# Graph transformer over adjacency lists: paced steps, a pair's contexts turned one at a time, an earlier request for zT, a later flag, products of ones at the start, a last tile in two column halves

## The chip, the core and the metric

The kernel runs on one core of one Trainium2 chip. The metric is the device time of one execution in microseconds (us). The engines named below are PE (TensorE, with PEld for its weight loads), DVE (VectorE), ACT (ScalarE), POOL (GpSimd) and SP, whose queue issues transfers.

## The reference

Two layers of a graph transformer over 2708 nodes with 512 features, 8 heads of 64 and an inner width of 2048, all in float32. A node attends only to its neighbours in `adj` and to itself.

```
mask = adj + eye(n)
q, k, v = split_heads(h @ Wq.T + bq), split_heads(h @ Wk.T + bk), split_heads(h @ Wv.T + bv)
scores = where(mask == 0, -1e9, q @ k.T / 8)
ctx = softmax(scores) @ v
h1 = layer_norm(h + ctx @ Wo.T + bo, ln1_g, ln1_b)
out = layer_norm(h1 + relu(h1 @ W1.T + b1) @ W2.T + b2, ln2_g, ln2_b)
```

About nine of 2708 entries are set in a row, so nearly all scores are masked.

## The kernel before

`by_edges` (from L469) does the work; `by_rows` is a dense version that runs only if a flag, computed on the chip, says that the lists did not suffice.

**Tiles and blocks.** The nodes are sorted by how many neighbours they have and cut into 22 tiles of 128 rows; the last, tile 21, has 20 rows. `blocks` pairs them: (20, 19), (18, 17), (8, 9) and so on to (1, 16) and (21, 0). `order` is the same list, flat.

**Stages.** First come keys and values of all tiles in layer 0 (`first`), while DVE, ACT and POOL find each row's neighbours in `adj` (`lists`). Then come the queries of layer 0 (`first_queries`), with the first attention steps beside them. Then, for each layer, the eleven blocks go through the feed-forward part (`feed_forward`); layer 0 also makes keys and values of layer 1 for a finished block (`keys_values`), and at the change of layers PE makes layer 1's queries (`queries`, `query`).

**Attention** (`attend`, L1563) runs on POOL, DVE and ACT. A step takes two neighbours (SLOTS) of all rows of a tile: POOL gathers their key and value rows (L1095); DVE multiplies the keys by the query row and reduces by head (L1132, L1138); one step later ACT takes the exponent (L1151) and scales values (L1158), and DVE adds them (L1164, L1171). Two steps after a tile's last one come its sums, and three after it ACT divides and writes the context `cx` (L1202); the tile's number then stands in `got`, which holds at most three (CXB). A step that needs a query row fetches it (`asked`): by a gather on POOL from `q_d` in layer 0, by SP in layer 1.

**The feed-forward of a block** has 16 slices f of the inner width. PE makes `pf` (L1488, eight passes; a float32 product is two passes) into one of three PSUM banks, ACT applies the ReLU into `ft` (L1499), and three slices later (LAG) PE adds that slice's product into `a` (L1461). Between the slices stand, for the next block: turning its two contexts (`attended`: a transpose `tp` on PE at L1268 and a copy `cT` on ACT), the output product `o`, the first norm on DVE with a power on POOL (`rd`, L1258), and turning the result into `hT` (`turned`). A 20-row tile's products run in four quarters of the array (L597, L1476).

**Order.** All five engines are scheduled by hand: each runs its instructions strictly in the order in which the program text makes them. What interleaves attention with the rest is a pace. `advance(more)` (L1628) adds `more` to a credit of at most 1.5 and makes steps, each costing about its slots over two, while the credit is above zero and `got` has room. The tables `PACE` and `PACES` (the latter for a layer's first block) give `more` for each f; it is 0 for the first two to four slices and for two slices near f=11, where contexts are turned and norms run. `through(k)` makes steps until both tiles of block k stand in `got`.

```
credit = min(credit + more, 1.5)
while credit > 0 and len(got) < CXB:
    cost = next(ahead, None)
```

**Around the change.** At t = NT - 7 of the layer-0 queries, both contexts of block 0 are turned, and at t = NT - 6 their output products follow. At the start of layer 1 both are turned, then one query is made, then the output products. In every block both contexts of the next one are turned at f=10 (12 in the very first). `queries` asks SP for up to three tiles' `zT` (the transposed layer input) ahead of a query; in layer 1's block 0 it asks for tiles 21 and 0 at f=0, and their queries come at f=3 and f=7. `cT` and `zT` share three buffers. In layer 1's last block `checked` (f=8) and `settled` (f=11 and f=14) gather the flag: a product with `ones` (L1622), a comparison into `redo`, and a read of `redo` into a register. In that block the products into `a` wait until all ReLUs are done (`apart`), tile 21 first and tile 0 last; then come the addition (L1520), the norm (L1252 to L1262) and the store of tile 0.

Of the kernel before, what the change touches and what calls it, by code (L numbers as in the profile page):

```python
# [8 lines left out]
F32 = mybir.dt.float32  # L9
# [4 lines left out]
ALU = mybir.AluOpType  # L14
# [4 lines left out]
P = 128  # L19
DM = 512  # L20
# [5 lines left out]
NFC = FF // P  # L26
# [8 lines left out]
Q4 = 32  # L35
# [7 lines left out]
AHEAD = 10  # L43
XB, XBS = 256, 11
LEAD = 1.2
QT = 16
OWN = 5
LISTS = (4, 7, 9, 12, 13, 14, 15, 17, 18, 19)
EARLY = 3
PACES = (  # L50
# [429 lines left out]
def by_edges(ctx: ExitStack, tc: tile.TileContext, x, xT, adj, layers, out, redo):  # L480
# [9 lines left out]
    nc = tc.nc  # L490
    N = x.shape[0]
    NT = (N + P - 1) // P
# [28 lines left out]
    make_identity(nc, ident)  # L521
    ones = const.tile([P, P], F32, name="ones")
    nc.gpsimd.memset(ones, 1.0)
    mhalf = const.tile([P, 1], F32, name="mhalf")
    nc.gpsimd.memset(mhalf, -0.5)
    listed = const.tile([P, NT, 2 * LIST], F32, name="listed")
# [89 lines left out]
    def finish(steps):  # L616
        for _ in steps:
            pass
# [627 lines left out]

    def norm(z, r, gain, shift):

        st = small.tile([P, 6], F32, tag="st", name="st")
        nc.vector.bn_stats(st[:r], z[:r])  # L1252
        mv = small.tile([P, 2], F32, tag="mv", name="mv")
        nc.vector.bn_aggr(mv[:r], st[:r])
        va = small.tile([P, 1], F32, tag="va", name="va")
        nc.vector.tensor_scalar(va[:r], mv[:r, 1:2], EPS, None, ALU.add)  # L1256
        rd = small.tile([P, 1], F32, tag="rd", name="rd")
        nc.gpsimd.tensor_tensor(rd[:r], va[:r], mhalf[:r], ALU.pow)  # L1258
        nc.vector.scalar_tensor_tensor(
            z[:r], z[:r], mv[:r, 0:1], gain[:r], ALU.subtract, ALU.mult  # L1260
        )
        nc.vector.scalar_tensor_tensor(z[:r], z[:r], rd[:r], shift[:r], ALU.mult, ALU.add)  # L1262
# [14 lines left out]
    class Layer:  # L1277
# [131 lines left out]
        def attended(self, block, got, xbs=None):  # L1409

            cTs, hs = [], []
            for g in block:
                r = size(g)
                cx = got.pop(g)
                cT = dn.tile([P, NC, P], F32, tag="cT", name="cT", bufs=3)
                flip(cx, r, cT[:, :, :r], self.bv)
                cTs.append((g, r, cT))
            xbs = xbs or self.residuals(block)
            yield
            for (g, r, cT), xb in zip(cTs, xbs):  # L1420
                o = project(lambda c: cT[:, c, :r], r, self.wo, "o")
                h = dn.tile([P, DM], F32, tag="h", name="h", bufs=4)
                nc.vector.tensor_tensor(h[:r], o[:r], xb[:r], ALU.add)  # L1423
                plus_rest(h[:r], o, r)
                if self.n == 0:
                    nc.vector.tensor_tensor(h[:r], h[:r], self.bo[:r], ALU.add)
                norm(h, r, self.g1, self.e1b2)
                hs.append(h)
                yield
            yield hs  # L1430
# [10 lines left out]
        def feed_forward(self, block, hs, hT):  # L1441
# [9 lines left out]
                ]  # L1451
                wide = [t.rearrange("p s (i w) -> p (s i) w", w=2 * P) for t in wide]

            def second(f, only=None):
                c0 = 0
                for g, a in zip(block, accs):
                    r = size(g)
                    if only not in (None, g) or r <= Q4:
                        c0 += r
                        continue  # L1460
                    nc.tensor.matmul(  # L1461
                        a[:r],
                        fts[f][:, c0 : c0 + r],
                        self.w2[f // 2][:, f % 2, :],
                        start=(f == 0),
                        stop=(f == NFC - 1),
                    )
                    c0 += r
# [44 lines left out]
            zs = []  # L1513
            for g, a, h in zip(block, accs, hs):
                r = size(g)
                if apart:
                    for f in range(NFC):
                        second(f, g)
                z = h
                nc.vector.tensor_tensor(z[:r], a[:r], h[:r], ALU.add)  # L1520
                plus_rest(z[:r], a, r)
                norm(z, r, self.g2, self.e2)
                if self.n == NL - 1:
                    put(out, ident_i[:r, g : g + 1], z[:r], "out")
                zs.append(z)
# [36 lines left out]
    now = Layer(0, layers[0])  # L1562
# [53 lines left out]
    def settled():  # L1616

        held = small.tile([P, 1], F32, tag="held", name="held", bufs=1)
        nc.vector.tensor_reduce(held, flags, AX.X, ALU.min)
        yield  # L1620
        pr = ps.tile([P, DM], F32, tag="g", name="pr")
        nc.tensor.matmul(pr[:1, :1], ones[:, :1], held, start=True, stop=True)  # L1622
        nc.vector.tensor_scalar(redo, pr[:1, :1], P - 0.5, None, ALU.is_lt)
        yield nc.values_load(redo[0:1, 0:1], min_val=0, max_val=1)

    credit = 0.0

    def advance(more):  # L1628

        nonlocal credit  # L1630
        credit = min(credit + more, 1.5)
        while credit > 0 and len(got) < CXB:
            cost = next(ahead, None)
            if cost is None:
                break
            credit -= cost

    def through(k):

        while blocks[k][-1] not in got:  # L1640
            next(ahead)

    got = {}
# [10 lines left out]
    def beside_queries(t):  # L1654

        if t in (8, 10, 12, 14):
            now.load_w1(t // 2 - 4, nc.gpsimd)
            now.load_w2(t // 2 - 4, nc.gpsimd)
        if t == 6:
            now.settle()  # L1660
        if t == 16:
            now.load_w1(4, nc.scalar)
            now.load_w2(4, nc.scalar)
        if t > OWN + 1:
            advance(0.65)
        if t == NT - 10:
            early[0] = now.residuals(blocks[0])
        if t == NT - 7:
            through(0)
            early[0] = now.attended(blocks[0], got, early[0])  # L1670
            next(early[0])
        if t == NT - 6:
            for _ in blocks[0]:
                next(early[0])
        if t == NT - 2:
            *_, early[0] = early[0]
            early[0] = early[0], now.turned(blocks[0], early[0])
# [6 lines left out]
    for n in range(NL):  # L1684
        last = n == NL - 1
        nxt = None if last else Layer(n + 1, layers[n + 1])
        if n > 0:
            streamed = now.queries(order[10:16])
            got = {}
            ahead = attend(n, got)  # L1690
            for _ in range(2):
                now.query(*pool.pop(0))
            next(ahead)
            both = now.two(order[8:10])
            pool += [(g, both[:, i]) for i, g in enumerate(order[8:10])]
            next(streamed)
            now.stores = nc.scalar
            while pool:
                if len(pool) < 5:
                    advance(0.65)  # L1700
                now.query(*pool.pop(0))
            for i, _ in enumerate(streamed):
                if i == 1:
                    both = now.two(order[16:18])
                if i == 4:
                    now.stores = nc.sync
                if len(got) < 2 or i < 3:
                    advance(0.65)
            through(0)
            early[n] = now.attended(blocks[0], got)  # L1710
            next(early[n])
            now.query(order[16], both[:, 0])
            for _ in blocks[0]:
                next(early[n])
            streamed = now.queries(order[18 : 2 * AHEAD])
            next(streamed)
            now.query(order[17], both[:, 1])
            advance(0.6)
            next(streamed)
            advance(0.6)  # L1720
            *_, hs = early[n]
            early[n] = hs, now.turned(blocks[0], hs)
            finish(streamed)
            now.apart = False
            now.load_w2(NFC // 2 - 1)
        hs, hT = early[n]
        projecting = xbs = None
        for k, block in enumerate(blocks):
            more = k + 1 < NB
            asking = iter(())  # L1730
            if n > 0 and k + AHEAD < NB:
                asking = now.queries(blocks[k + AHEAD])
            for f, zs in enumerate(now.feed_forward(block, hs, hT)):
                if f == NFC:
# [3 lines left out]
                if more and n == 0 and f == 5 + 2 * (k == 0):  # L1738
                    xbs = now.residuals(blocks[k + 1])
                if more and f == 10 + 2 * (k + n == 0):  # L1740
                    through(k + 1)
                    projecting = now.attended(blocks[k + 1], got, xbs)
                    xbs = None
                    next(projecting)
                if more and f == 11 + 2 * (k + n == 0):
                    *_, hs_next = projecting
                if more and f == NFC - 1:
                    finish(asking)
                    hT = now.turned(blocks[k + 1], hs_next)
                advance((PACE if k else PACES)[n][f])  # L1750
                if f in (0, 3, 7, 9):
                    next(asking, None)
                if k == 0 and len(now.w1) < NFC // 2 and f % 2 == 0:
                    now.load_w1(len(now.w1), nc.scalar)
# [2 lines left out]
                    now.load_second(1, temp)  # L1757
                if last and not more and f == 8:
                    checked()
                if last and not more and f == 11:  # L1760
                    settling = settled()
                    next(settling)
                if last and not more and f == 14:
                    again = next(settling)
                if not more and f == 0:
                    finish(ahead)
# [99 lines left out]
```

## Time and profile before

| | |
|---|---|
| median of 3 runs | 1864.73 us (1863.62 to 1865.01) |
| the profiled execution's own time | 1866.47 us |
| its span, first to last instruction | 1864.4 us |
| mean granted PE clock | 0.994 |
| DMA, mean over the span | 197 GB/s |

The profile shows one execution. Its groups give a line, an engine, an operation, the tiles written and read, a count, the busy time and the mean of one. A PE row's duration reaches until its result is out, while the next product starts earlier: passes of 512 columns start 0.43 us apart and are listed with 0.59 us each. The waits view sums, for an engine, what ended its idle time. The windows view gives busy time, the granted clock and DMA of a stretch. Where the names are not enough, the timeline gives each instruction's start, duration and, in brackets, the idle time before it and its releaser.

### The profile page before, as it was taken

To read this page: it belongs to the slowest core of one execution; us is meant where nothing else is said; L and a number is where in the kernel's file an instruction comes from. 1 tells how busy PE (TensorE), PEld (TensorE's weight loads), DVE (VectorE), ACT (ScalarE), POOL (GpSimd) and SP (SyncE) were. 2 spreads that over 40 slices of the span, in tenths; PEclk is the share of its full clock that TensorE was granted. 3 is DMA by queue.
4 is the path that set the end of the run, shared out by engine and by line. 5 is a ranking of instruction groups with operands and counts; after the bars stand their busy time and mean duration, and the time that the engine had idled before them with its cause. 6 is when DMAs were issued, how large, how long until landed. Compare 5 with 4: busy or idle time off the path is not lost.

```text
span 1864.4 us, 20896 instructions
## 1 busy us (share of the span) xinstructions
PE 1833.7 (98%) x6149; PEld 1088.4 (58%) x6149; DVE 1373.0 (74%) x2145; ACT 944.3 (51%) x3263; POOL 778.2 (42%) x745
## 2 busy tenths in 40 slices
PE   9999989999999999999999999999999999999997
PEld 3444446665656656566565644566666666666664
DVE  5886868777776867768674147878988998899842
ACT  5770535555555555455553113655655675666521
POOL 3234754443444534435430032434453654455302
PEclk9999989999999999999999999999999999999999
DMA  9997977545554565444631676826554664565300
GB/s 343 363 338 257 362 256 254 191 151 207 183 173 154 183 199 183 156 169 133 218 120 45 228 263 239 318 101 226 187 187 175 241 222 143 201 211 175 119 1 20
DMA packets 129829, 368.01 MB, mean 197 GB/s; under 512 B 14378, under 2 KB 32670, under 8 KB 129704
## 3 DMA queue, kind: packets, MB, share of 16 engines
q0 software_dynamic: 70608, 252.12, 39.4%
q1 hardware_dynamic: 50042, 93.64, 14.3%
q10 hardware_dynamic: 9054, 20.81, 2.9%
q8 instruction: 50, 0.82, 0.2%
q14 instruction: 75, 0.61, 0.1%
HBM read 315.84 MB, written 50.68 MB: 197 GB/s over the span
## 4 chain that ended last, share of the span: by engine, by line
PE 92%; DVE 3%; DMA 2%; issue 2%; ACT 1%; POOL 0%; ACTq 0%; SPq 0%; POOLq 0%; DVEq 0%
PE pf L1488 31%; PE a L1461 31%; PE k L602 8%; PE v L602 8%; PE o L602 7%; PE q L602 4%; PE tp L1268 3%; PE a L1476 1%; DMA kv<-kv_d,listed 1%; DMA zT<-zT_d 1%; DVE kv L1132 0%; DVE sc L1138 0%; DMA q_d<-qs 0%; ACT kv L1158 0%; ACT cx L1202 0%
## 5 line engine op out<-in xcount | busy, mean ns | idle before, releaser
L1488 PE MATMUL pf<-hT,w 128*128 128x256 f32 (+1 forms) x2816 | 635.2, 373 | 10.0 <-ACT ft L1499 9.1
L1488 PEld LDWEIGHTS pf<-hT,w 128*128 128x128 f32 x2816 | 520.1, 191 | 185.1 <-issue 107.3
L1461 PE MATMUL a<-w,ft 128*128 128x512 f32 x1312 | 611.3, 592 | 0.0
L1095 POOL DMA_INDIRECT kv<-kv_d,listed x420 | 501.8, 1195 | 260.0 <-issue 111.9
L1499 ACT ACTIVATE ft<-pf,b 128x256 f32<-128x256 f32 (+1 forms) x336 | 153.8, 461 | 432.9 <-PE pf L1488 427.9
L1461 PEld LDWEIGHTS a<-w,ft 128*128 128x128 f32 x1312 | 247.2, 190 | 187.8 <-issue 166.7
L1258 POOL TENSOR_TENSOR rd<-va,mhalf 128x1 f32<-128x1 f32 (+1 forms) x88 | 81.4, 925 | 577.4 <-DVE va L1256 577.3
L1158 ACT ACTIVATE kv<-kv,p 128x64 f32<-128x64 f32 x1232 | 311.0, 335 | 5.0
L1132 DVE TENSOR_TENSOR kv<-kv,q 128x1024 f32<-128x1024 f32 (+1 forms) x222 | 257.1, 1158 | 10.6 <-DMA q<-q_d,ident_i 7.6
L1138 DVE TENSOR_REDUCE sc<-kv 128x16 f32<-128x1024 f32 (+1 forms) x222 | 258.0, 1162 | 7.6
L1171 DVE TENSOR_TENSOR acc<-acc,kv 128x1024 f32<-128x1024 f32 (+2 forms) x178 | 205.3, 1153 | 75.8 <-ACT kv L1158 61.4
L1151 ACT ACTIVATE p<-sc,listed 128x8 f32<-128x8 f32 x420 | 104.7, 300 | 143.9 <-DVE sc L1138 114.5
L1164 DVE TENSOR_TENSOR kv<-kv,p 128x512 f32<-128x512 f32 (+1 forms) x178 | 122.6, 689 | 60.2 <-ACT p L1151 45.2
L602 PE MATMUL o<-wo,cT 128*128 128x512 f32 x336 | 148.0, 593 | 0.0
L602 PEld LDWEIGHTS o<-wo,cT 128*128 128x128 f32 x336 | 63.7, 190 | 81.1 <-issue 76.6
L727 DVE MAX8 tops<-code 128x8 f32<-128x247 f32 (+2 forms) x242 | 78.6, 400 | 28.9 <-ACT code L722 28.7
L1262 DVE SCALAR_TENSOR_TENSOR h<-h,rd,ln_b 128x512 f32<-128x512 f32 (+1 forms) x88 | 66.1, 751 | 42.2 <-POOL rd L1258 42.2
L1202 ACT ACTIVATE cx<-acc,su 128x64 f32<-128x64 f32 (+1 forms) x352 | 88.3, 333 | 13.2 <-DVE su L1194 7.4
L1158 ACT ACTIVATE acc<-kv,p 128x64 f32<-128x64 f32 (+1 forms) x352 | 88.8, 335 | 1.4
L602 PE MATMUL k<-wk,xg 128*128 128x512 f32 x168 | 78.0, 608 | 4.6 <-DMA wk<-in_Wk 4.6
L722 ACT ACTIVATE code<-aj 128x1354 bf16<-128x1354 int32 (+1 forms) x44 | 72.8, 1720 | 18.9 <-POOL aj L716 13.4
L1423 DVE TENSOR_TENSOR h<-o,xb 128x512 f32<-128x512 f32 (+1 forms) x44 | 30.2, 686 | 62.7 <-PE o L602 38.9
(179 smaller groups left out, 1524.4 us busy)
## 6 DMA issues: line engine op xcount, KB each, us to landing
aj<-in_adj SPq DMA_DIRECT2D x42, 677.0 KB
kv_d<-kvs ACTq DMA_DIRECT2D x21, 512.0 KB
xg<-in_xT SPq DMA_DIRECT2D x19, 512.0 KB
w<-in_W SPq DMA_DIRECT2D x16, 512.0 KB
kv<-kv_d,listed POOLq DMA_INDIRECT x420
zT_d<-zT SPq DMA_DIRECT2D x22, 256.0 KB
xb_d<-h SPq DMA_DIRECT2D x21, 256.0 KB
q<-q_d SPq DMA_DIRECT2D x21, 256.0 KB
```

Of the source, the lines that this page charges most:

```text
L602: nc.tensor.matmul(o[:r], xs(c), wm[:, c, :], start=(c == 0), stop=(c == NC - 1))
L1095: return nc.gpsimd.indirect_dma_start(out=to, out_offset=None, in_=table[:, :], in_offset=bass.IndirectOffsetOnAxis(ap=s, axis=0), bounds_ ...
L1132: nc.vector.tensor_tensor(kv[:r, :c, :DM], kv[:r, :c, :DM], self.q[:r].unsqueeze(1).to_broadcast([r, c, DM]), ALU.mult,)
L1138: nc.vector.tensor_reduce(self.sc[:r, s0 : s0 + c, :], kv[:r, :c, :DM].rearrange("p s (h d) -> p s h d", d=DK), AX.X, ALU.add,)
L1151: nc.scalar.activation(p[:r, s, :], self.sc[:r, s, :], AF.Exp, bias=minus[:r, g, s : s + 1])
L1158: nc.scalar.activation(to[:, i, hd], kv[:r, i, DM + h * DK : DM + (h + 1) * DK], AF.Copy, scale=p[:r, s0 + i, h : h + 1],)
L1164: nc.vector.tensor_tensor(to[:, 0, :].rearrange("p (h d) -> p h d", d=DK), kv[:r, 0, DM:].rearrange("p (h d) -> p h d", d=DK), p[:r, s0, : ...
L1171: nc.vector.tensor_tensor(self.acc[:r, :c, :], self.acc[:r, :c, :], kv[:r, :c, DM:], ALU.add)
L1202: nc.scalar.activation(cx[:r, hd], self.acc[:r, 0, hd], AF.Copy, scale=self.su[:r, h : h + 1])
L1461: nc.tensor.matmul(a[:r], fts[f][:, c0 : c0 + r], self.w2[f // 2][:, f % 2, :], start=(f == 0), stop=(f == NFC - 1),)
L1488: nc.tensor.matmul(pf[:, :w], self.w1[f // 2][:, c, f % 2 * P : f % 2 * P + P], hT[:, c, :w], start=(c == 0), stop=(c == NC - 1),)
L1499: nc.scalar.activation(ft[:, :w], pf[:, :w], AF.Relu, bias=self.b1[:, f : f + 1])
```

## The change

Seven edits. `advance` returns at once for a pace of 0, so that left-over credit makes no step there. `through(k)` becomes `until(g)`, for one tile, and `attended` yields after each of its two turns: the first context is turned at f=10 (12), the second one slice later, directly ahead of the output products. In layer 0's queries the first is turned at t = NT - 8, and the second and the output products at NT - 7; at the start of layer 1 one query comes between the two turns. The request for `zT` of tiles 21 and 0 moves ahead of the query of tile 16, which precedes the feed-forward. The flag's reduction moves from f=11 to f=10, its product from f=14 to f=12, and the read stays at f=14. Twelve products of `ones` with itself are put ahead of the keys. The very last tile's products are made in two halves of 256 columns, each with its own addition and statistics.

```
+WARM = 12
...
+    pr = ps.tile([P, DM], F32, tag="g", name="pr")
+    for _ in range(WARM):
+        nc.tensor.matmul(pr[:, :P], ones, ones, start=True, stop=True)
...
-    def norm(z, r, gain, shift):
+    def norm(z, r, gain, shift, st=None):
-        st = small.tile([P, 6], F32, tag="st", name="st")
-        nc.vector.bn_stats(st[:r], z[:r])
+        if st is None:
+            st = small.tile([P, 6], F32, tag="st", name="st")
+            nc.vector.bn_stats(st[:r], z[:r])
...
                 cTs.append((g, r, cT))
-            xbs = xbs or self.residuals(block)
-            yield
+                if g == block[0]:
+                    xbs = xbs or self.residuals(block)
+                yield
...
-                if apart:
-                    for f in range(NFC):
-                        second(f, g)
+                if apart and r > Q4:
+                    st = small.tile([P, 2, 6], F32, tag="st2", name="st2", bufs=1)
+                    for i in range(2):
+                        cols = slice(i * DM // 2, (i + 1) * DM // 2)
+                        for f in range(NFC):
+                            second(f, g, cols)
+                        nc.vector.tensor_tensor(z[:r, cols], a[:r, cols], h[:r, cols], ALU.add)
+                        nc.vector.bn_stats(st[:r, i], z[:r, cols])
...
         nc.vector.tensor_scalar(redo, pr[:1, :1], P - 0.5, None, ALU.is_lt)
+        yield
         yield nc.values_load(redo[0:1, 0:1], min_val=0, max_val=1)
...
     def advance(more):
+        if not more:
+            return
...
-    def through(k):
-        while blocks[k][-1] not in got:
+    def until(g):
+        while g not in got:
             next(ahead)
...
-        if t == NT - 7:
-            through(0)
+        if t == NT - 8:
+            until(blocks[0][0])
             early[0] = now.attended(blocks[0], got, early[0])
             next(early[0])
-        if t == NT - 6:
+        if t == NT - 7:
+            until(blocks[0][1])
+            next(early[0])
             for _ in blocks[0]:
                 next(early[0])
...
             next(early[n])
             now.query(order[16], both[:, 0])
+            until(blocks[0][1])
+            next(early[n])
...
             early[n] = hs, now.turned(blocks[0], hs)
+            asking = now.queries(blocks[AHEAD])
+            next(asking)
             finish(streamed)
...
                 if more and f == 10 + 2 * (k + n == 0):
-                    through(k + 1)
+                    until(blocks[k + 1][0])
                     projecting = now.attended(blocks[k + 1], got, xbs)
...
                     next(projecting)
                 if more and f == 11 + 2 * (k + n == 0):
+                    until(blocks[k + 1][1])
                     *_, hs_next = projecting
...
-                if f in (0, 3, 7, 9):
+                if f in (0, 3, 7, 9) and (f or k):
                     next(asking, None)
...
-                if last and not more and f == 11:
+                if last and not more and f == 10:
                     settling = settled()
-                    next(settling)
-                if last and not more and f == 14:
+                if last and not more and f in (10, 12, 14):
                     again = next(settling)
```

More of the change, by code (lines that the diff above doesn't have):

```diff
@@ L1452, in feed_forward, with second @@
                 wide = [t.rearrange("p s (i w) -> p (s i) w", w=2 * P) for t in wide]
-            def second(f, only=None):
+            def second(f, only=None, cols=slice(0, DM)):
                 c0 = 0
@@ L1461, in second @@
                     nc.tensor.matmul(
-                        a[:r],
+                        a[:r, cols],
                         fts[f][:, c0 : c0 + r],
-                        self.w2[f // 2][:, f % 2, :],
+                        self.w2[f // 2][:, f % 2, cols],
                         start=(f == 0),
@@ L1515, in feed_forward @@
                 r = size(g)
-                if apart:
-                    for f in range(NFC):
-                        second(f, g)
[L1519 to L1522, printed above, removed]
+                z, st = h, None
+                if apart and r > Q4:
[6 more added lines that the diff above has]
+                        nc.vector.bn_stats(st[:r, i], z[:r, cols])
+                else:
+                    nc.vector.tensor_tensor(z[:r], a[:r], h[:r], ALU.add)
+                    plus_rest(z[:r], a, r)
+                norm(z, r, self.g2, self.e2, st)
                 if self.n == NL - 1:
@@ L1708, in by_edges @@
                     advance(0.65)
-            through(0)
+            until(blocks[0][0])
             early[n] = now.attended(blocks[0], got)
@@ L1729, in by_edges @@
             more = k + 1 < NB
-            asking = iter(())
-            if n > 0 and k + AHEAD < NB:
+            if k or n == 0:
+                asking = iter(())
+            if n > 0 and 0 < k < NB - AHEAD:
                 asking = now.queries(blocks[k + AHEAD])
```

## Prediction

> **What bounds the kernel now.** I read the page first: TensorE (PE) is busy for nearly the whole span.
>
> ```profile
> span 1864.4 us, 20896 instructions
> PE 1833.7 (98%) x6149; PEld 1088.4 (58%) x6149; DVE 1373.0 (74%) x2145; ACT 944.3 (51%) x3263; POOL 778.2 (42%) x745
> ```
>
> The change adds a few products and removes none, so it can gain only where PE stands still or runs slowly. Second, what PE waited for (total us, times, longest):
>
> ```profile
> PE pf L1488 <- ACT ft L1499: 9.1, 1, 9.1
> PE k L602 <- DMA wk<-in_Wk: 4.6, 1, 4.6
> PE tp L1268 <- ACT cx L1202: 2.9, 4, 1.3
> PE q L597 <- DMA zT<-zT_d: 2.7, 1, 2.7
> PE pf L1488 <- ACT fts L1499: 0.8, 1, 0.8
> ```
>
> Third, the same places in stages (length, PE, PEld, DVE, ACT, POOL busy, granted clock, DMA share, GB/s): after three of the waits PE goes on at half clock.
>
> ```profile
> 268.60:272.20 3.60, 3.54 (x8) 2.86 (x9) 3.56 (x7) 0.72 (x3) 2.52 (x4) 0.50 1.00 324
> 1144.00:1147.50 3.50, 1.81 (x9) 0.91 (x8) 2.32 (x6) 2.20 (x10) 0.00 (x0) 1.00 0.35 124
> 1180.50:1184.00 3.50, 3.50 (x13) 1.59 (x14) 3.43 (x5) 0.00 (x0) 2.57 (x2) 0.56 1.02 383
> 1214.20:1217.70 3.50, 3.50 (x10) 2.72 (x9) 2.06 (x3) 3.47 (x15) 0.00 (x0) 0.51 0.00 0
> ```
>
> Fourth, the largest wait in order of time, PE and then ACT, POOL, DVE:
>
> ```profile
> 257.66 1.88 PE L1461 MATMUL a<-w,ft 128*128 128x512 f32 x4
> 268.66 3.74 PE L1488 MATMUL pf<-hT,w 128*128 128x256 f32 x8 [9.12 <-ACT ft L1499]
> ...
> 273.95 1.89 PE L1488 MATMUL pf<-hT,w 128*128 128x256 f32 x8
> ```
> ```profile
> 252.68 0.47 ACT L1499 ACTIVATE ft<-pf,b 128x256 f32<-128x256 f32 x1 [1.31 <-PE pf L1488]
> ...
> 265.70 0.49 ACT L1151 ACTIVATE p<-sc,listed 128x8 f32<-128x8 f32 x2 [12.36 <-DVE sc L1138]
> ...
> 268.15 1.17 ACT L1499 ACTIVATE ft<-pf,b 128x256 f32<-128x256 f32 x3
> ```
> ```profile
> 259.67 1.01 POOL L1095 DMA_INDIRECT q<-q_d,ident_i  x1 [2.58 <-DMA bq<-in_bq]
> ```
> ```profile
> 263.19 1.23 DVE L1132 TENSOR_TENSOR kv<-kv,q 128x1024 f32<-128x1024 f32 x1 [7.56 <-DMA q<-q_d,ident_i]
> ```
>
> After slice f=0 of the first feed-forward the pace is 0, but left-over credit made two attention steps. They need tile 17's query row, gathered at 259.67 and there at 263.19. ACT, in order, stands at their exponent until 265.70, the ReLUs of f=1 to 3 behind it, and PE has no free pf bank.
>
> **Part by part.**
>
> *Zero pace.* In the changed program's order the two steps come after f=4, so ACT reaches the exponent behind ft of f=4. PE then runs on from 250.65: 1.73 us a slice for f=0 to 2, 3.45 from f=3 (273.95 to 277.39), so pf of f=4 ends at 261.0, of f=5 at 264.5. With the gather unmoved, ft of f=5 starts at 268.15, 3.7 late. By the same rows ft of f=6 comes after DVE's next reduction (269.3), 0.5 exponent, 2.0 scaling and 2.0 for cx: 273.9, 6.0 late; f=10 I find about 7 late. A ReLU may start 8.1 late before PE waits: three banks, so 3x1.72 + 2x1.73 until the bank is wanted, less 0.47. So no wait, with 1 us of margin. Gain 9.12 + (3.74 - 1.89) = 10.97. Two things move the gather: the weight DMAs of f=0 and f=2 are no longer held behind ACT: four of 512 KB, issued at 266.31 to 267.88 before, now go at about 253 to 256 beside the q_d stores, 2.1 MB at 385 GB/s, up to 5.4 us later; against that the norms of tiles 20 and 19 now precede a step's gathers on POOL, where DVE idled 2.83 us for rd (237.78), so the last q_d store leaves up to 2 us sooner. I keep 0.5 us of wait: -10.5, ends -11 and -5. Elsewhere a step slips by about one slice. Nothing waits for it: by the order both contexts of the next pair stand in `got` at f=10 of every block but layer 1's first, and the turn itself comes at f=10 and 11.
>
> *Contexts turned apart.* At layer 1's start PE turned tile 20, waited for tile 19's cx, then made a query; now the query (3.43) lies between. Wait 1.24 and a slow turn (1.76 for 0.60): -2.4. Its cover is that query; without it the 2.4 return. At t=15 of layer 0 the cT copy loses its cover: +0.2. In layer 1's block 0 both turns stood at f=10: they took 3.51 (1210.57 to 1214.08) for 0.88, then 3.40 for 1.89 and 2.10 for 1.88 at half clock, 4.36 lost. Now f=11's 3.45 lie between, but the first cT copy comes ahead of cx of tile 17 on ACT: 0.3 + 1.06 copy + 0.49 exponent + 2.02 + 2.0 cx + 0.1 = 5.97 from the first turn, against PE's 0.45 + 3.45 + 0.45 = 4.35: 1.6 still waited. Half clock may follow (+1.7) or not. I take 2.3 left: -2.1, ends -4.3 and 0. In other blocks cx is done a slice or more before.
>
> *zT sooner.* Wait 2.67, then 1.92 for 1.05 and 2.60 for 1.89 at half clock: 4.25. Both zT left SP at 1170.83 behind two q_d stores and 512 KB of weights. Now they follow the store that went at 1162.53; the second needs the slot that query 1 frees (PE, 1164.7). Even with the 9.6 us that the chain gives this DMA, the first lands by 1172.1, the second by 1174.3, and PE, 2.4 earlier, wants the first at 1175.4. SP holds two q_d stores and w2 behind that slot, whose evictions come at about that time anyway: 0. -4.2.
>
> [...]
>
> *Products of ones.* Twelve 128x128 products, 24 passes; ones is ready at 1.52, the first wk at 4.63. In the chain the first key tile's eight passes take 6.04, the next ones' 3.43; the rows between are half rate, with 0.85 between passes until 9.40. 24 passes at 0.218 (half of 512 columns' rate, 429 ns, is 0.858) last 5.1: to 6.9, or 6.5 if the clock comes sooner; they delay the keys by about 2 and spare the 2.4 to 2.6 that half rate costs. [...] -0.5, ends -1.5 and +0.8.
>
> *Flag later.* The 0.77 at 1838.44 is PE reading redo just after making it; now two slices lie between. -0.6, ends -0.8 and 0. Its product at f=12 waits for held, done at 1827.0.
>
> *Halves of the last tile.* The add and statistics after the last product go from 0.69 to an estimated 0.42 each (0.54 between the 512 and 1024 column adds, halved): -0.54. 64 passes at 0.216 for 32 at 0.429: +0.1. [...] +0.3, ends -0.4 and +0.8.
>
> Sum: -10.5 - 2.4 + 0.2 - 2.1 - 4.2 - 0.5 - 0.6 + 0.3 = -19.8. The profiled execution is 1866.47 (span 1864.4): 1846.7. It lies 1.7 above the median of 1864.73, so the median becomes 1844.9.
>
> **Rivals.** *The first wait moves instead of going.* For: ACT still stands at the same exponent, the 2.1 MB go earlier, and margins are 1 us. If the gather lands 5 us later, ReLUs f=6 and 10 start 11 to 12 late: about 4 us of waits, with clock 5 in all: 1850. Against: DVE's stores leave earlier. *Everything goes*, no residue at either place and a good clock window: 1841. *The change doesn't do what it says*: zT stays behind SP's store and the credit is spent elsewhere; the waits return one slice on: 1864. Against: the order shows both moved. *Slower:* DVE and ACT, relieved of nothing, now trail a PE that is 15 us ahead; two steps fall on the first paid slice (2 x 4.2 us of DVE) in every block. It decides once a ReLU is over 8.1 late. Two steps (1.16 + 1.16 + 0.69 + 1.15 each, by the groups of L1132, L1138, L1164 and L1171) on a ReLU that is 1 late make 9.4, so 1.3 of wait, in 18 blocks 23 us: 1844.9 + 23 = 1868. Against: the latest I found outside the first block are 6.3, with key products in between, and 5.9 (pf to 1645.4, the cx of 1649.34 before the ReLU); every block's start and end are back at 0.2, and the order doubles steps in few places.
>
> **Numbers.** Forecast 0.68 at 1844.9 (its own 1842 to 1848); moved wait 0.20 at 1850; all gone 0.07; no change 0.02; slower 0.03. Range 1841 to 1851. A measurement can tell 0.2%, 3.7 us: faster 0.95, same 0.02, slower 0.03.
>
> **What would show it.** No PE wait over 1 us in the first feed-forward and no half clock there; zT's wait gone; cx's left once, near 1.6, at layer 1's first f=11; one new wait of PE for DVE in the last tile; the first key tile near 3.6 but starting near 6.5. Wrong if waits for ft appear at f=6 to 10 or in later blocks.

## The result, and the profile after

| | before | changed |
|---|---|---|
| median | 1864.83 us (4 runs, one more than above) | 1847.65 us (1846.59, 1846.72, 1848.58, 1848.60) |
| profiled execution | 1866.47 us | 1846.72 us |
| its span | 1864.4 us | 1844.6 us |
| ratio of the medians | | 0.9909, 95% interval 0.9892 to 0.9926 |

The change makes the kernel 17.2 us faster. The profiled execution lies where the prediction's sum put it (1846.7); the median is 2.7 us above the 1844.9 that was made of it, inside the range. The page of the changed kernel, its first lines:

```profile
span 1844.6 us, 20998 instructions
PE 1830.8 (99%) x6205; PEld 1095.4 (59%) x6205; DVE 1374.6 (75%) x2147; ACT 944.3 (51%) x3263; POOL 782.5 (42%) x745
```

PE's waits in the changed kernel (total us, times, longest). Of the five lines of before, those for `ft` (9.1), `zT` (2.7) and `fts` (0.8) are gone; `cx` is left once with 0.7, and the wait for `wk` has become one for `ones` and 0.4 for `wk`. New are `cT` and L1529.

```profile
PE pr L527 <- POOL ones L524: 1.6, 1, 1.6
PE tp L1273 <- ACT cx L1206: 0.7, 1, 0.7
PE o L606 <- ACT cT L1278: 0.6, 1, 0.6
PE tp L1273 <- DVE h L1267: 0.6, 1, 0.6
PE a L1467 <- DVE h L1529: 0.5, 1, 0.5
PE k L606 <- DMA wk<-in_Wk: 0.4, 1, 0.4
```

The windows view of the same three places: the first feed-forward, the query of tile 21 and the second turn of layer 1's block 0. Its columns are length, busy time of PE, PEld, DVE, ACT and POOL, granted clock, DMA share and GB/s. The clock is 1.00 in all.

```profile
268.60:272.20 3.60, 3.60 (x14) 2.36 (x13) 3.53 (x8) 2.75 (x12) 2.83 (x3) 1.00 1.01 366
1163.50:1167.00 3.50, 3.50 (x19) 1.96 (x18) 3.36 (x5) 1.67 (x8) 2.46 (x3) 1.00 1.03 400
1196.00:1200.00 4.00, 2.87 (x9) 1.16 (x8) 1.23 (x2) 3.94 (x17) 0.00 (x0) 1.00 0.00 0
```

From here on, "lost" is counted on PE from the trace: the time from the start of one pass to the start of the next, less what such a pair of passes usually takes (0.429 us for 512 columns, 0.216 for 256). It holds waits, half clock and slow turns together.

The first feed-forward loses nothing in this execution, but by a hair. ACT reaches the exponent of the two steps at 261.57 and gets the scores at 266.66; the ReLUs trail from there on (timeline of the changed kernel, ACT):

```profile
261.20 0.47 ACT L1505 ACTIVATE ft<-pf,b 128x256 f32<-128x256 f32 x1 [3.03 <-PE pf L1494]
261.57 0.29 ACT L1155 ACTIVATE p<-sc,listed 128x8 f32<-128x8 f32 x1
266.66 0.49 ACT L1155 ACTIVATE p<-sc,listed 128x8 f32<-128x8 f32 x2 [4.80 <-DVE sc L1142]
...
290.13 0.46 ACT L1505 ACTIVATE ft<-pf,b 128x256 f32<-128x256 f32 x1
```

And PE:

```profile
290.20 0.60 PE L1273 MATMUL tp<-ident,cx 128*128 128x128 f32 x4
290.64 1.99 PE L1494 MATMUL pf<-hT,w 128*128 128x256 f32 x8
```

The ReLU of f=10 ends at 290.59 (the start and duration of its row above), and the slice f=13, which needs its bank, starts at 290.64.

### The profile page after: what moved, and what is told of

Same layout as the page of the kernel before. It is cut to its first block, busy times and chain, and to the rows that moved or that the text cites. A ratio compares the mean times of both kernels' runs of the same rounds, so it can differ in the third digit from the quotient of the medians.

```text
span 1844.6 us, 20998 instructions
## 1 busy us (share of the span) xinstructions
PE 1830.8 (99%) x6205; PEld 1095.4 (59%) x6205; DVE 1374.6 (75%) x2147; ACT 944.3 (51%) x3263; POOL 782.5 (42%) x745
## 4 chain that ended last, share of the span: by engine, by line
PE 93%; DVE 3%; ACT 1%; issue 1%; DMA 1%; POOL 0%; SPq 0%; POOLq 0%; DVEq 0%
PE pf L1494 30%; PE a L1467 29%; PE o L606 8%; PE v L606 8%; PE k L606 8%; PE q L606 7%; PE tp L1273 3%; DVE sc L1142 1%; DVE kv L1136 1%; PE a L1482 1%; ACT kv L1162 1%; DVE acc L1175 0%; DVE kv L1168 0%; ACT cx L1206 0%; DMA kv<-kv_d,listed 0%
## 5 line engine op out<-in xcount | busy, mean ns | idle before, releaser
L1099 POOL DMA_INDIRECT kv<-kv_d,listed x420 | 507.8, 1209 | 254.2 <-issue 108.7
L1560 ACT COPY kvs<-v 128x512 f32<-128x512 f32 (+1 forms) x22 | 12.9, 585 | 137.3 <-PE v L606 136.6
```

The source lines that it names most:

```text
L1099: return nc.gpsimd.indirect_dma_start(out=to, out_offset=None, in_=table[:, :], in_offset=bass.IndirectOffsetOnAxis(ap=s, axis=0), bounds_ ...
```

## The experiments

Unless it says otherwise, each kernel is the changed one with the edit shown. Since the same kernel differs by 1 to 4 us between executions, the places in the traces tell more than the medians.

**The changed kernel once more.** 

> The changed kernel itself once more, as what the other runs of this chip are to be compared with. Expected 1846.5 to 1849, 0.991 of before. Its profile is expected to show in the first feed-forward what the time tells: no PE wait there with a time near 1846.6, and a wait for ft of 1 to 2 with one near 1848.6.

Measured: 1848.16 us (1847.30 to 1851.03, 4 runs), 0.9899 of before (0.9885 to 0.9914). Its profiled execution, the one of 1851.03, lost 4.10 in the first feed-forward, more than expected. Its span is 4.4 longer than that of the first profile (1849.0 against 1844.6): 4.1 of this lies here, while the first value product comes 0.45 later. From POOL, DVE and PE of its timeline:

```profile
260.67 1.01 POOL L1099 DMA_INDIRECT q<-q_d,ident_i  x1 [4.63 <-DMA raw<-in_bo]
...
267.99 1.22 DVE L1136 TENSOR_TENSOR kv<-kv,q 128x1024 f32<-128x1024 f32 x1 [13.41 <-DMA q<-q_d,ident_i]
...
279.08 2.58 PE L1494 MATMUL pf<-hT,w 128*128 128x256 f32 x8 [1.90 <-ACT ft L1505]
```

Its windows, before and after the clock fell:

```profile
276.93:280.35 3.42, 1.52 (x7) 1.15 (x7) 3.28 (x5) 3.39 (x15) 0.99 (x1) 1.00 0.92 328
280.35:283.76 3.41, 3.41 (x7) 1.84 (x6) 3.27 (x5) 2.02 (x8) 2.65 (x3) 0.50 0.60 190
```

The same rows of the first execution, for comparison:

```profile
258.81 1.01 POOL L1099 DMA_INDIRECT q<-q_d,ident_i  x1 [4.20 <-DMA w<-in_W]
...
264.14 1.23 DVE L1136 TENSOR_TENSOR kv<-kv,q 128x1024 f32<-128x1024 f32 x1 [10.82 <-DMA q<-q_d,ident_i]
```

In the same program, the gather of tile 17's query row left 9.8 instead of 8.3 us after the feed-forward's first product (250.84 and 250.48) and took 7.3 instead of 5.3 to the multiplication that needs it. That is the rival "the first wait moves", and the wait of 1.90 stands at f=9, where the prediction's sign of being wrong has it (waits for ft at f=6 to 10).

**Later weights.** In layer 0's first block:

```
-                if k == 0 and len(now.w1) < NFC // 2 and f % 2 == 0:
+                if k == 0 and len(now.w1) < NFC // 2 and f % 2 == 0 and f > 3:
```

> The changed kernel with the three pairs of weight loads of layer 0's first block issued behind ft of f=4, 6 and 8 instead of f=0, 2 and 4. Theory (the two groups of the changed kernel's times, 2.0 us apart, come from its first feed-forward, where the ReLU of f=10 is 8.5 late with 0.1 to spare, and the weights' transfers beside tile 17's q_d store and gather set by how much): the gather leaves up to 1.5 us and lands up to 3.3 us sooner against the start of the feed-forward, the ReLU of f=10 is at most 7 late, no PE wait and no half clock there, all times in the lower group: median -1 to -2 on the changed kernel. Rival (the groups come from the clock at the head or at layer 1's turn): times as before in two groups, median unchanged. Rival 2: a later weight is itself waited for at f=10 or 12, slower by 1 or more.

Measured: 1846.09 us (1845.73 to 1847.30), 0.9889 of before (0.9875 to 0.9904); on the same chip the changed kernel has 1848.16. The median gains 2.1, about what the theory has, though the two intervals overlap, and the times lie within 1.6. The profiled execution, the slowest of them, does not show all that was expected: its last `q_d` store left 5.5 us after the first product (DVE was late), the gather 4.2 behind it and the multiplication 4.7 behind the gather. With the early weights these legs were 5.5 and 5.3 in one execution, 6.1 and 7.3 in the other. So the transfers were quicker, but the store was later, the ReLU of f=10 came 8.9 late and 0.48 was lost behind it (and 0.35 at f=3, whose cause the trace does not name).

The table puts these rows of all traces side by side, in us behind the feed-forward's first product.

| trace | last `q_d` store | gather leaves | multiplication | lost in the first feed-forward |
|---|---|---|---|---|
| before | 5.0 | 9.0 | 12.5 | 11.13 (steps behind f=0) |
| zero pace undone | 3.8 | 8.1 | 11.6 | 10.41 (steps behind f=0) |
| zero pace alone | 2.9 | 8.4 | 13.6 | 0 |
| changed | 2.9 | 8.3 | 13.7 | 0 |
| tail as before | 2.9 | 8.5 | 13.7 | 0.16 |
| eight products of ones | 2.9 | 8.4 | 13.8 | 0.25 |
| other bank, turn at f=12 | 2.9 | 8.3 | 13.9 | 0.36 |
| no products of ones | 3.8 | 10.0 | 15.3 | 1.74 |
| turns together | 3.7 | 9.9 | 15.7 | 1.64 |
| `zT` back | 3.8 | 10.0 | 17.2 | 4.10 |
| changed, once more | 3.8 | 9.8 | 17.2 | 4.10 |
| slower first block | 3.8 | 9.5 | 16.0 | 1.24 |
| later weights | 5.5 | 9.7 | 14.4 | 0.83 |
| all at once (with later weights) | 2.9 | 7.3 | 10.8 | 0 |

The eight rows from "changed" to "changed, once more" have the same program at this place ("turns together" differs shortly ahead of it, at t = 15). Among them, a multiplication at 13.7 to 13.9 costs 0 to 0.4, one at 15.3 to 15.7 costs 1.6 to 1.7, one at 17.2 costs 4.1. Two things set when it comes.

The first is the weights' transfers. With the store at 3.8, the multiplication came at 11.6 where ACT issued the weights only after the gather (zero pace undone, from 264.77), and at 15.3 to 17.2 where they went early. With the store at 2.9, it came at 10.8 with later weights and at 13.6 to 13.9 with early ones.

The second is the store. It leaves at 2.9 or at 3.8, and where it leaves at 3.8 the row lands 1.4 to 3.5 later. This is decided before the feed-forward: the power `rd` of tile 20's norm starts on POOL 19.7 us ahead of the first product in the five traces of the changed order with the store at 2.9, 18.4 ahead in the five with 3.8, and 16.7 ahead in the one with 5.5 ("turns together" and "zero pace alone" have another order there). In POOL's program `rd` stands behind gathers, and in the changed kernel's second profile one of them (`xb`, at 219.54) took 1.89 where it took 1.00 in the first. Why it took longer is not shown.

This is the likeliest reason why the first four times of the changed kernel form two groups 2.0 apart. For those very executions it is argued, since only one has a trace, and the four times of its second run form no such groups.

**A slower first block.** The pace of layer 0's first block is 0.7 instead of 0.85 for f=4 to 11. 

> The changed kernel with the pace of layer 0's first block at 0.7 instead of 0.85 for f=4 to 11. Theory (as in the run with the later weights: the first feed-forward has no margin): a step's 4.2 us of DVE times 0.7 is 2.9 a slice where PE takes 3.45, so the lag of 7 that the gather leaves falls by about 0.5 a slice, to some 4 at f=10, and no wait is left: -1 to -2 on the changed kernel. Rival (contexts then come too late and PE waits for cx or cT at f=12 or in later blocks): +1 or more.

Measured: 1848.96 us (1848.24 to 1852.99), 0.9909 of before (0.9897 to 0.9922). The theory did not hold: the ReLU of f=10 was 4.0 late, as worked out, but that of f=6 was 9.2 late, before the pace can help, and 1.24 was lost at f=9. The rival held; contexts came later in all of layer 0, and PE waited for `cT` in three places, one of them that of the changed kernel (waits of this kernel):

```profile
PE o L606 <- ACT cT L1278: 2.1, 3, 1.2
```

**Zero pace undone.** `if not more: return` is taken out. 

> The changed kernel with one part undone: a pace of 0 lets left-over credit make steps again. Theory: the wait for ft of about 9 us at the first feed-forward is back with half clock behind it, +10.5 to +11.1, 1858.4, and nothing else moves by over 0.5. Rival (the other edits, the earlier turns of layer 0 among them, had already taken part of that wait): +3 to +8, 1851 to 1856.

Measured: 1856.67 us (1856.15 to 1859.25), 0.9957 of before (0.9944 to 0.9971). The wait is back in its trace, with half clock behind it, 10.41 lost in all:

```profile
267.12 3.78 PE L1494 MATMUL pf<-hT,w 128*128 128x256 f32 x8 [8.21 <-ACT ft L1505]
```

Nothing else moved by over 0.8. By the ratios the median is 9 to 11 above the changed kernel's two, and that kernel loses 0 to 4 here itself.

**Zero pace alone**, put into the kernel before. 

> The kernel before with one part of the change alone: a pace of 0 makes no step. Theory (the wait for ft of the first feed-forward goes by this edit alone): -9 to -11 on the kernel before, less the 0 to 4 that the changed kernel's own first feed-forward lost in three of four other profiles: 1856.5, 0.9955 of before. Rival (it needs the earlier turns as well): under -5, 1860 or more.

Measured: 1856.76 us (1851.84 to 1858.81), 0.9942 of before (0.9929 to 0.9956), 10.2 less than the 1866.91 of before on that chip. Its trace loses nothing in the first feed-forward. The edit takes the wait away by itself.

**`zT` asked for at f=0 again.** 

> The changed kernel with one part undone: zT of tiles 21 and 0 is asked for at f=0 of layer 1's first block again. Theory (wait and half clock): PE waits 2.7 for zT, the granted clock falls to about half behind it, +4.2, 1851.9. [...]

Measured: 1850.22 us (1849.81 to 1855.08), 0.9920 of before (0.9906 to 0.9934). The wait is back, and this time the clock stayed. Timeline and windows:

```profile
1172.43 1.05 PE L601 MATMUL q<-wq,zT 128*20 128x512 f32 x8 [2.89 <-DMA zT<-zT_d]
```
```profile
1168.06:1171.48 3.42, 1.48 (x4) 0.38 (x2) 3.28 (x5) 2.57 (x10) 2.21 (x2) 1.00 1.04 410
1171.48:1174.89 3.41, 2.46 (x15) 1.46 (x16) 3.34 (x5) 0.00 (x0) 2.49 (x2) 1.00 1.03 372
```

PE lost 3.48 here against 0.52 in the changed kernel: 2.96, about the wait alone (2.89). In the kernel before, 2.67 of wait had cost 4.59. Why the price differs stands in the last section.

**Turns together.** Both yields and calls of `until` are put back at one place everywhere. 

> The changed kernel with one part undone: both contexts of a pair are turned at one place again, everywhere. Theory: layer 1's start +2.4, layer 1's block 0 loses 4.36 instead of 2.01 (+2.3), the wait of output products for cT at 1327 goes (-0.9), t = 15 of layer 0 -0.2; sum +3.6, 1851.3. Rival (what is lost in layer 1's block 0 hangs on when cx is made and not on where the first turn stands): only layer 1's start returns, +1.5, 1849.1.

Measured: 1851.02 us (1849.33 to 1853.64), 0.9926 of before (0.9912 to 0.9939). By the trace: layer 1's start lost 4.03 against 0.19, its block 0 2.65 against 2.01, the wait for `cT` at 1327 is gone (0.87), t = 15 gets 0.18 better. Sum +3.4, near the theory's 3.6, but made up differently: at the start the same two waits brought half clock, which they had not in the kernel before, and in block 0 they did not (the eight passes of `pf` at 1200.98 take 1.89), which they had there.

```profile
1135.35 1.76 PE L1273 MATMUL tp<-ident,cx 128*128 128x128 f32 x4 [1.04 <-ACT cx L1206]
```
```profile
1134.40:1137.82 3.42, 2.03 (x7) 0.99 (x8) 1.37 (x3) 3.12 (x13) 0.00 (x0) 1.00 0.61 225
1137.82:1141.23 3.41, 3.41 (x6) 1.32 (x5) 0.00 (x0) 0.94 (x4) 0.00 (x0) 0.50 0.65 210
```

**No products of ones.** 

> The changed kernel without the twelve products of ones. Theory (the products spare the keys their half rate and cost about as much): the first value product starts near 10.7 instead of 10.28, time +0.4 on 1847.65, 1848.1. Rival 1 (the products fill what they win with waste, and hold the first key tile back): -0.8, 1846.8. Rival 2, for the changed kernel's times in two groups 2.0 us apart (1846.6 and 1848.6): the phase of the clock's window against the early products makes them; then this kernel's times stand in one group, within 1 us. If the groups come from somewhere else, they are here as well.

Measured: 1848.62 us (1846.72, 1848.13, 1849.12, 1849.42), 0.9908 of before (0.9893 to 0.9923). The median does not tell it from the changed kernel. The times spread over 2.7, so times this far apart do not need the early products. The first value product starts at 11.52.

**Eight products of ones.** 

> The changed kernel with eight products of ones instead of twelve. Theory (sixteen passes at half rate last 3.4, from 1.59 to 5.0, and the first wk is there at 4.7): the first key product starts near 5.0 instead of 5.96, and the first value product 0 to 0.9 sooner than 10.28, less where the transfers of wk and wv bind. Rival (with fewer products the clock comes a window later): first value product at 10.7 or later.

Measured: 1847.45 us (one run). The keys start at 5.16 and the values at 9.76, though the first eight passes of the keys take 4.54, those of the values 3.60:

```profile
5.16 4.54 PE L606 MATMUL k<-wk,xg 128*128 128x512 f32 x8
...
9.76 3.60 PE L606 MATMUL v<-wv,xg 128*128 128x512 f32 x8
```

Over all traces the first value product starts at 10.72, 11.31 and 11.52 without such products (mean 11.2), at 9.70 to 10.85 with twelve (nine traces, mean 10.3), at 9.76 and 9.33 with eight (mean 9.5).

**The tail as before:** last tile in one piece, flag at f=11 and 14. 

> The changed kernel with both edits of its last block undone: the last tile's products in one piece, the flag made at f=11 and read at f=14. Read from the start of the last block's first slice to the end of the span, against the same stretch of the changed kernel. Theory (the prediction's terms): PE waits 0.8 for redo again and no longer for the first half's addition; the stretch is 0.6 - 0.3 = 0.3 longer. Rival (the halves win more at the end than their wait costs): 0.8 or more longer. Rival 2 (two passes of 256 columns cost more than one of 512): shorter.

Measured: 1847.51 us (one run). From the first quarters' products of the last block (L1482) to the end it takes 1802.41 to 1845.5, 43.1; the changed kernel takes 42.7 (from 1801.93), the kernel before 43.1 (from 1821.29). The two edits gain 0.4 together, 0.3 expected.

**Another bank, and the second turn at f=12** in layer 1's first block, with the steps still made at f=11:

```
...
+                        if i:
+                            a = ps.tile([P, DM], F32, tag="g", name="a2")
                         for f in range(NFC):
-                            second(f, g, cols)
+                            second(f, g, cols, a)
...
                 if more and f == 11 + 2 * (k + n == 0):
                     until(blocks[k + 1][1])
+                if more and f == 11 + 2 * (k + n == 0) + (n > 0 and k == 0):
                     *_, hs_next = projecting
```

> The changed kernel with two edits far apart in time. In the last tile the second half's products go into another PSUM bank, so that they wait for nothing: theory, the wait of PE for the first half's addition (0.78 lost) goes and the end comes 0.8 sooner after the last block's start; rival, a pause at the change of banks stays. In layer 1's first block the second turn and the output products stand at f=12, with the steps still made at f=11: theory, the 2.0 lost on cx of tile 17 near 1198 go, as a slice of 3.45 covers the rest of the 5.97 from the first turn to cx; rival, cx comes a slice later too, and 2 are lost at f=12.

Measured: 1843.42 us (one run). Both theories hold: the second turn waits for nothing, the 64 passes of the last tile run as one group, and the stretch to the end is 41.9 (from 1799.45), 0.8 shorter.

```profile
1199.44 0.60 PE L1273 MATMUL tp<-ident,cx 128*128 128x128 f32 x4
...
1818.48 14.08 PE L1467 MATMUL a<-w,fts 128*128 128x256 f32 x64
```

**All at once:** later weights, the other bank, the turn at f=12, eight products of ones. 

> The changed kernel with what the runs so far point to, all at once: later weight loads in layer 0's first block, the last tile's second half in another PSUM bank, the second turn of layer 1's first block at f=12, eight products of ones. Theory: 2.0 (later weights, measured) + 2.0 + 0.8 + 0.3 below the changed kernel: 0.987 of before, about 1842 to 1843. Rival (the waits are taken up by others, as at the first feed-forward): no better than the later weights alone, 0.989.

Measured: 1843.03 us (1842.43 to 1843.69), 0.9878 of before (0.9862 to 0.9895), below both kernels. No wait in its first feed-forward, at layer 1's turn or in the last tile; PE's waits are these:

```profile
PE pr L527 <- POOL ones L524: 1.6, 1, 1.6
PE o L606 <- ACT cT L1278: 0.6, 1, 0.6
PE tp L1273 <- DVE h L1267: 0.6, 1, 0.6
PE k L606 <- DMA wk<-in_Wk: 0.3, 1, 0.3
```

## Why the prediction held, point by point

The terms of the sum, against the two profiled executions:

| step | predicted | measured | from |
|---|---|---|---|
| zero pace | -10.5 | -11.1 | lost 11.13, then 0 |
| layer 1's start | -2.4 | -2.4 | lost 2.56, then 0.19 |
| t = 15 | +0.2 | +0.2 | lost 0.53, then 0.71 |
| layer 1's block 0 | -2.1 | -2.3 | lost 4.33, then 2.01 |
| other blocks' turns | 0 | +0.9 | 0.87 lost at 1327 |
| `zT` sooner | -4.2 | -4.1 | lost 4.59, then 0.52 |
| products of ones | -0.5 | -0.4 | first value product at 10.72, then 10.28 |
| flag and halves | -0.3 | -0.5 | 43.15, then 42.67 to the end |
| sum | -19.8 | -19.7 | span 1864.4, then 1844.6 |

*Zero pace.* The mechanism held: the steps came behind f=4, PE ran on from the first slice, and ACT stood at the same exponent. The ReLUs were 4.7 late at f=5 (3.7 predicted), 6.9 at f=6 (6.0) and 8.5 at f=10 (about 7), each 0.9 to 1.5 larger, because the multiplication came at 264.14 and not at the 263.19 that was kept. The two opposing effects did not cancel: the store left 2.1 sooner, counted from the first product, but the way from store to gather grew from 4.0 to 5.5 and from gather to multiplication from 3.5 to 5.3. The margin of 1 us shrank to less than 0.1, and that was luck: 8.5 late is over the 8.1 that the prediction allowed, and it cost nothing only because the turn's transposes (0.44), which the 8.1 did not count, stand between f=12 and f=13.

*Why the median is higher.* "I keep 0.5 us of wait" was the mis-sized term. The eight traces with this place unchanged (the rows named under the table) lost 0 to 4.10, on average 1.5. The profiled one lost none. So the likeliest case and the rival "the first wait moves" (1850) both occur, in different executions of one program; that rival was given 0.20, and with half clock it made 1851.03. The second part of the gap is the step from profile to median: the 1.7 between them was carried over, but it belonged to one execution, and the changed kernel's profile lies 0.9 below its median. The kernel before had medians of 1864.83, 1865.42, 1866.91 and 1865.36 on the chips of these runs.

*Contexts.* Predicted was 5.97 from the first turn to `cx` of tile 17 against PE's 4.35, and 2.3 left. The rows show it, PE and then ACT of the changed kernel:

```profile
1192.59 0.60 PE L1273 MATMUL tp<-ident,cx 128*128 128x128 f32 x4
1193.03 1.89 PE L1494 MATMUL pf<-hT,w 128*128 128x256 f32 x8
1194.76 1.88 PE L1467 MATMUL a<-w,ft 128*128 128x512 f32 x4
1197.33 1.76 PE L1273 MATMUL tp<-ident,cx 128*128 128x128 f32 x4 [0.69 <-ACT cx L1206]
```
```profile
1193.23 1.14 ACT L1278 ACTIVATE cT<-tp,bv 128x128 f32<-128x128 f32 x4 [1.68 <-DMA xb<-xb_d]
1194.24 0.51 ACT L1155 ACTIVATE p<-sc,listed 128x8 f32<-128x8 f32 x2
1194.78 2.02 ACT L1162 ACTIVATE kv<-kv,p 128x64 f32<-128x64 f32 x8
1196.70 2.00 ACT L1206 ACTIVATE cx<-acc,su 128x64 f32<-128x64 f32 x8
```

The wait was shorter than 1.6, since the four transposes did not wait for all eight of ACT's divisions: they start at 1197.33, 1197.81, 1198.28 and 1198.76, about 0.06 after every second division ends. But so the turn went at ACT's pace (1.76 for 0.60): 2.01 in all. These ACT rows follow one another without idle time, so it is ACT's own work, the copy first, that sets when `cx` is done; with the turn at f=12, one slice later, it was done in time (no wait at 1199.44).

*What was missed:* "In other blocks cx is done a slice or more before" looked at `cx` only. With the second turn directly ahead of the output products, its `cT` copy no longer has a slice to get through ACT, and at 1327, where ReLUs are 6 to 7 late, PE waits for it. ACT there:

```profile
1324.44 2.02 ACT L1162 ACTIVATE kv<-kv,p 128x64 f32<-128x64 f32 x8
1326.36 0.45 ACT L1505 ACTIVATE ft<-pf,b 128x256 f32<-128x256 f32 x1
1326.72 1.11 ACT L1278 ACTIVATE cT<-tp,bv 128x128 f32<-128x128 f32 x4
```

*`zT`* came in time, as predicted, but what the wait had cost hangs on the clock: 4.1 against this profile of before (0.50 in the window behind it), 3.0 against the run with the request back (1.00).

*Products of ones.* The sum was right in the profiled pair (-0.4). Its parts were not: the keys started at 5.96 where 6.5 was expected, and their first tile took 4.3, not 3.6. Over all traces the gain is 0.9, inside the range. Eight products do better (9.5 against 10.3, by two traces): the keys start at 5.0 to 5.2 instead of 5.8 to 6.9, and PE waits for no `wk` at that start.

*Flag, halves.* The wait for `redo` went. Beside its -0.54 and +0.1, the +0.3 of the halves holds about 0.74 for a wait of the second half for DVE's addition, which was the author's estimate and which no run on record then showed; in the changed kernel this wait came, and 0.78 was lost. PE's row of the second half:

```profile
1828.65 7.17 PE L1467 MATMUL a<-w,fts 128*128 128x256 f32 x32 [0.52 <-DVE h L1529]
```

The rival of a slower kernel did not come true: outside the first block no ReLU is over 6.7 late, and PE waits for none.

## What to carry to other kernels

When a wait of one engine is removed by letting it run ahead, work out the margin of what trails behind it in every execution and not in one: here a margin of 0.05 us turned into 0 to 4 us of loss as a row landed up to 3.5 us later in another execution. Look for transfers that were held behind the old wait and leave earlier without it: here, with the store at 2.9, the multiplication that everybody waits for came at 13.6 to 13.9 with early weights and at 10.8 with later ones (the run with all at once). When two turns are taken apart, look for cover behind each as well, for the copy that follows (0.87 lost at 1327).

## What the runs showed of the chip

In the traces of the kernel before and of the changed one the records of the granted clock change at multiples of 3.413 us from one another (before: 272.226, 1180.171, 1183.584, 1214.304, and 907.945 is 266 times 3.413; changed: 4.941 and 1837.898, 537 times). Such a stretch of 3.413 is called a window here. The table sets how busy PE was in a window beside the clock of the next. Each pass counts here from its start with its time at full clock (0.429 for 512 columns, fewer in proportion), at most until the next one starts, and only windows at full clock stand in the table. The views' PE column counts a pass until its result is out and shows more: the 1.52 of 3.42 at 276.93 and the 1.48 of 3.42 at 1168.06 above are 0.36 and 0.39 of a window by starts.

| busy share of a window, by starts | clock of the next window | where |
|---|---|---|
| 0.22, 0.26 | half | before, at 1210.89 and 1176.76 |
| 0.36, 0.38 | half | changed once more at 276.93, turns together at 1134.40 |
| 0.39, 0.39 | full | `zT` back at 1168.06, zero pace undone at 257.42 |
| 0.41 | full | changed, at 1196.19 |
| 0.59 | full | before, at 1142.62: the wait at 1144, where the prediction's stages have full clock |

The other windows of before and changed agree: half clock follows shares of 0 to 0.34 (the long wait of the first feed-forward, and the end of each), full clock follows 0.45 and more. The highest share with half clock behind it is 0.38 and the lowest with full clock 0.39, by one window and two: that is what these executions did, and no more is shown. A wait of 1.9 brought half clock in one execution (280.35 above) and one of 2.9 none in another (1171.48 above); the first fell into one window and the second across two. So a prediction that takes half clock from one profile takes what one execution did: the wait for `zT` cost 4.59 in the kernel before, with half clock behind it, and 2.96 with the request back, without.
